# Self-attention of an adaLN cross block: adding the two chunks of weights on VectorE before the sum over keys

## The chip, the cores and the metric

The kernel runs on one core of one Trainium2 chip. The metric is the device time of one execution in microseconds (us); three runs of the kernel before gave 2964.05 us as their median, with 2962.16 and 2967.8 at the ends.

## The reference

All tensors are float32. There are B = 16 sequences of N = 224 tokens, width H = 512, 16 heads of 32, and a context of 750 tokens for each sequence. Cut to what matters:

```python
shift_a, scale_a, gate_a, shift_m, scale_m, gate_m = split(silu(c) @ W_mod + b_mod, 6)
x_norm = _ln(x) * (1 + scale_a) + shift_a
q, k, v = split(x_norm @ W_qkv + b_qkv, 3)              # 16 heads of 32
attn_w = softmax(einsum('bhqd,bhkd->bhqk', q, k) * scale)
attn_out = einsum('bhqk,bhkd->bhqd', attn_w, v)         # heads joined to 512
x = x + gate_a * (attn_out @ W_proj + b_proj)
# then cross-attention to the context, with weights softmax(q_c k_c^T),
x = x + (softmax(...) @ v_c) @ W_cproj + b_cproj
# then the MLP of width 2048
x = x + gate_m * (gelu((_ln(x)*(1+scale_m)+shift_m) @ W_mlp1 + b_mlp1) @ W_mlp2 + b_mlp2)
```

The change is in the softmax of the self-attention: `attn_w` is never formed. The kernel multiplies the unnormalised exponentials by `v`, sums them over the keys apart from that, and divides the first by the second.

## The kernel before, in words

The kernel has three stages that follow one another: self-attention (to about 770 us of the profiled span), cross-attention (to about 2290 us) and the MLP.

**Self-attention.** The 16 sequences go in 8 pairs `p`, and the 16 heads in 4 groups `g` of 4 heads (a group fills 128 rows of queries or keys, 32 for each head). A unit is one pair, one group and one sequence `j` of the pair, so there are 64 units. Keys lie on partitions, in TC = 2 chunks of TP = 112, and the 224 queries along the free dimension. For each unit:

1. `self_scores`: TensorE makes the scores with queries on partitions, VectorE takes the maximum of each query (`m`, one reduction over 112x1792) and splits it into bfloat16 parts (`split_max`, four small instructions, tile `nm`). `max_rows` turns them on TensorE, and VectorE copies the result (`mrow`).
2. `self_weights` (through `weights_t`): TensorE makes the scores again, now with keys on partitions, less the maximum, in PSUM tile `sc`. ScalarE takes the exponential into `pt`, 112 partitions x 4 heads x (2 chunks x 224 queries).
3. `self_values`: `values` multiplies `pt` by `v` with 8 matmuls of 32 columns (2 chunks x 4 heads) into the left half of PSUM tile `o`; `sums` multiplies `pt` by ones with another 8 such matmuls into its right half, so that every one of a head's 32 rows holds the sum over the keys.
4. `finish` (`normalize`): VectorE takes the reciprocal of the sums into `rinv` and multiplies the left half of `o` by it into `at`, which the projection reads.

Steps 2 to 4 run one unit behind step 1. In program order, one turn of the loop is: scores of this unit; `finish` of the unit two back; slot 0 of the plan; weights of the unit one back; `max_rows`; slot 1 of the plan; values and sums of the unit one back. The plan, a table keyed by pair, unit and slot, puts the projections of the next pair (`project_qk`, `project_v`, `turn_x`), the output projection of the pair before (`project`) and the norms between these steps. `sc` exists once (4 banks of PSUM), `o` once, `mm` three times, `pt` twice. Every instruction goes through `Ordered`, so each engine's instructions stand in the order in which the program issues them. All of them carry line 28 in the profile, the line of that helper, and are told apart by their tiles.

In pairs 0 to 6 a slot mostly holds 8 float32 matmuls. The last pair has no next pair to project for, and its plan spreads what is left in `halves`: slots there hold 4 or 8 matmuls.

`project` reads a `gate` tile, which `gate_rows` loads over SyncE's queue when a sequence's first chunk is projected; VectorE adds the bias (`upd`), and GpSimd multiplies by the gate and adds to `x`. The pool has 3 buffers of `gate` before.

**Cross-attention** runs similar units with 6 chunks of 125 keys. There GpSimd already adds all chunks into one tile `acc` (`Unit.weights`), and `sums` is called with that tile alone, so it is 4 matmuls. It uses `normalize` too. **The MLP** uses `gate_rows` with 3 buffers.

Of the kernel before, what the change touches and what calls it, by code (L numbers as in the profile page):

```python
# [8 lines left out]
F32 = mybir.dt.float32  # L9
BF16 = mybir.dt.bfloat16  # L10
AF = mybir.ActivationFunctionType
ALU = mybir.AluOpType
# [25 lines left out]
def kernel(  # L38
# [23 lines left out]
    nc = Ordered(tc)  # L62
    B, N, H = x.shape
    S = context.shape[1]
    MLP = w_mlp1.shape[1]
    P = 128
# [4 lines left out]
    HG = P // HD  # L71
    TP = 112
    TC = N // TP
    CP = 125
    CC = S // CP
# [5 lines left out]
    PN = PB * N  # L81
# [6 lines left out]
    NW = MLP // H  # L88
    NT = 3
    SCALE = float(HD) ** -0.5  # L90
    assert N == TC * TP and S == CC * CP and PN <= 512 and TC * N <= 512


    const = ctx.enter_context(tc.tile_pool(name="const", bufs=1))
# [19 lines left out]
    for i in range(3):  # L114
        t = const.tile([TP, TC, HG, HD], BF16, name=f"nm{i}")
# [86 lines left out]
                self.stats(i)  # L202
            self.apply()

    def gate_rows(pool, which, lo, n):

        g = pool.tile([n, H], F32, name="gate", bufs=3)
        at = lo
        while at < lo + n:
            b = at // N  # L210
            to = min((b + 1) * N, lo + n)
            nc.sync.dma_start(out=g[at - lo : to - lo, :], in_=gate_d[which][b].partition_broadcast(to - at))
            at = to
        return g

    def add_to_x(pool, ps, x_ap, bias, gate):
        r = ps.shape[0]
        t = pool.tile([r, H], F32, name="upd", bufs=2)
        nc.vector.tensor_tensor(t, ps, bias, ALU.add)
        if gate is not None:  # L220
            nc.gpsimd.tensor_tensor(t, t, gate, ALU.mult)
        nc.gpsimd.tensor_tensor(x_ap, x_ap, t, ALU.add)

    def project_heads(ps, a_t, w, lo):
        for g in range(KC):
            mm(ps[:TP, :H], a_t[g][:, lo : lo + TP], w[:, g, :], start=(g == 0), stop=(g == KC - 1))
            if g == 1:
                yield
# [6 lines left out]
    sa = self_pools.enter_context(tc.tile_pool(name="sa", bufs=3))  # L235
# [20 lines left out]
    for i in range(2):  # L256
        lo = (2 + 3 * i) * H
# [64 lines left out]
    def max_rows(pool, psum, nm):  # L322

        ps = psum.tile([P, 1024], BF16, name="mm")
        for c in range(TC):
            turn(ps[:, c * TP : (c + 1) * TP], nm[:, c].rearrange("p s d -> p (s d)"), ident16[:TP, :TP])
        row = pool.tile([P, N], BF16, name="mrow", bufs=2)
        nc.vector.tensor_copy(row, ps[:, :N])
        return row

    def weights_t(pool, psum, row, q_ap, k_ap, chunks, rows, bufs):

        st = psum.tile([P, HG, 512], F32, name="sc")
        n = len(chunks)
        for s in range(HG):
            mm(
                st[:rows, s, : n * N].rearrange("p (k t) -> p k t", k=n),
                ones16[s * HD : s * HD + NT, :rows],
                row[s * HD : s * HD + NT, :].unsqueeze(1).to_broadcast([NT, n, N]),
                start=True, stop=False,  # L340
            )
        for j, kc in enumerate(chunks):
            for s in range(HG):
                mm(
                    st[:rows, s, j * N : (j + 1) * N], k_ap(s, kc), q_ap(s),
                    start=False, stop=(j == n - 1),
                )
        pt = pool.tile([rows, HG, n * N], F32, name="pt", bufs=bufs)
        nc.scalar.activation(pt, st[:rows, :, : n * N], AF.Exp)
        return pt  # L350

    def values(o, pt, v_ap, chunks, rows, first):

        for j, kc in enumerate(chunks):
            for s in range(HG):
                mm(
                    o[s * HD : (s + 1) * HD, :N], v_ap(s, kc), pt[:, s, j * N : (j + 1) * N],
                    start=(first and j == 0), stop=False, skip_group_check=True,
                )

    def sums(o, pts, rows):

        for i, pt in enumerate(pts):
            for s in range(HG):
                mm(
                    o[s * HD : (s + 1) * HD, N : 2 * N], ones[:rows, :HD], pt[:, s, :],
                    start=False, stop=(i == len(pts) - 1), skip_group_check=True,
                )

    def normalize(pool, o, dst):  # L370
        rinv = pool.tile([P, N], F32, name="rinv", bufs=1)
        nc.vector.reciprocal(rinv, o[:, N : 2 * N])
        nc.vector.tensor_tensor(dst, o[:, :N], rinv, ALU.mult)

    def value_bias(pool, psum, w, vec, o_v, name):

# [9 lines left out]
    def run(plan, key):  # L386
        for f in plan.pop(key, ()):
            f()
# [19 lines left out]
    def load_ctx(b, hf):  # L408
        for c in range(hf * CH, (hf + 1) * CH):
            t = cw["cx"].tile([CP, H], F32, name="cx")  # L410
            nc.sync.dma_start(out=t, in_=context[b, c * CP : (c + 1) * CP, :])
            cx[b, c] = t
        ts = [cx[b, c] for c in range(hf * CH, (hf + 1) * CH)]
        cnorms[b, hf] = Norm(ts, ts, CP)
# [20 lines left out]
    if True:  # L435
# [6 lines left out]
        gate = {}  # L442
# [29 lines left out]
        def fetch(p):  # L472
            for b in range(PB * p, PB * (p + 1)):
                xs[b] = load_x(sa, tokens(x, b), 6)
# [15 lines left out]
        def project(p, t):  # L490
            b, c = PB * p + t // TC, t % TC
            if c == 0:
                gate[b] = gate_rows(sa, 0, b * N, TP)
            ps = ps_mm.tile([P, 512], F32, name="mm")
            yield from project_heads(ps, at[p], wproj, t * TP)
            add_to_x(sa, ps[:TP, :H], xs[b][:, c, :], bproj, gate[b])
            if c == TC - 1:
                nc.sync.dma_start(out=x_self[b], in_=xs[b])
# [7 lines left out]
        for p in range(NP):  # L506
# [23 lines left out]
            n = p + 1  # L530
# [35 lines left out]
        def self_weights(p, g, j, row):  # L566
            return weights_t(
                sa, ps_s, row,
                lambda s: qk[p, g][s * HD : (s + 1) * HD, j * N : (j + 1) * N],
                lambda s, kc: qk[p, KC + g][  # L570
                    s * HD : (s + 1) * HD, j * N + kc * TP : j * N + (kc + 1) * TP
                ],
                range(TC), TP, 2,
            )

        def self_values(p, g, j, pt):
            o = ps_o.tile([P, 512], F32, name="o")
            values(
                o, pt, lambda s, kc: vs[p, j * TC + kc][:, (g * HG + s) * HD : (g * HG + s + 1) * HD],
                range(TC), TP, True,  # L580
            )
            sums(o, [pt[:, :, c * N : (c + 1) * N] for c in range(TC)], TP)
            if g == 0 and j == 0:
                at[p] = []
            if j == 0:
                at[p].append(sa.tile([P, PN], F32, name="at", bufs=2 * KC))
            return lambda: normalize(sa, o, at[p][g][:, j * N : (j + 1) * N])
# [19 lines left out]
        was = None  # L607
        finish = None
        for i, (p, g, j) in enumerate(units):
            u = g * PB + j  # L610
            nm = nms[i % 3]
            self_scores(p, g, j, nm)
            if finish:
                finish()
            run(plan, (p, u, 0))
            if was:
                pt = self_weights(*was, row)
            row = max_rows(sa, ps_mm, nm)
            run(plan, (p, u, 1))
            if was:  # L620
                finish = self_values(*was, pt)
            was = (p, g, j)

            left = len(units) - i
            if left == 16:
                for hf in range(2):
                    load_ctx(0, hf)
                for c in range(TC):
                    first[c] = cw["mx"].tile([P, H], F32, name="mx")
                    nc.sync.dma_start(out=first[c][:TP], in_=x_self[0][:, c, :])  # L630
            if left in (10, 8):
                cnorms[0, left == 8].all()
            if left in (7, 6):
                Norm([first[7 - left][:TP]], [first[7 - left][:TP]], TP).all()
        finish()
        self_values(*was, self_weights(*was, row))()
        for t in range(PT):
            whole(project(NP - 1, t))
        assert not plan
# [163 lines left out]
    with tc.tile_pool(name="ca", bufs=2, reuse_waits="tile") as ca:  # L803
# [98 lines left out]
        for b in range(B):  # L902
            n = b + 1
# [52 lines left out]
        class Unit:  # L956
# [103 lines left out]
            def finish(self):  # L1060
                t = ca.tile([P, N], F32, name="at", bufs=2 * KC)
                normalize(ca, self.o, t)
                at.setdefault(self.b, []).append(t)
# [60 lines left out]
    with tc.tile_pool(name="ml", bufs=3, reuse_waits="tile") as ml:  # L1124
# [9 lines left out]
        resid = {}  # L1134
# [16 lines left out]
        def fetch(i):  # L1151
            t = ml.tile([P, H], F32, name="xr")
            q, lo = divmod(i * P, GR)
            nc.sync.dma_start(out=t, in_=x_cross[q][lo : lo + P, :])
            resid[i] = t, gate_rows(ml, 1, i * P, P)

        with (
            tc.tile_pool(name="ml_p", bufs=2, space=PSUM, reuse_waits="tile") as ps_p,
# [146 lines left out]
```

## Time and profile before

| | us |
|---|---|
| median of three runs | 2964.05 |
| lowest and highest | 2962.16, 2967.8 |
| the profiled execution, its time | 2967.63 |
| the profiled execution, its span | 2965.8 |
| TensorE matmuls busy | 2877.7 |
| VectorE busy | 1843.2 |
| ScalarE busy | 1175.4 |
| GpSimd busy | 1289.0 |

The span runs from the first to the last instruction; the execution's own time is 1.83 us longer, and lies 3.6 us above the median of the three runs. PE is TensorE's matmuls, PEld its weight loads, DVE VectorE, ACT ScalarE, POOL GpSimd, SP SyncE. A row of instructions gives the tile written, the tiles read, the shapes, the count, the busy time and the mean duration of one. A float32 matmul leaves two records, so 8 matmuls are shown as x16. In the timeline the first column is the start and the second the time until the last of the merged instructions ended; a bracket gives the idle time of the engine before it and what ended that.

### The profile page before, as it was taken

To read this page: it belongs to the slowest core of one execution; us is meant where nothing else is said; L and a number is where in the kernel's file an instruction comes from. 1 tells how busy PE (TensorE), PEld (TensorE's weight loads), DVE (VectorE), ACT (ScalarE), POOL (GpSimd) and SP (SyncE) were. 2 spreads that over 40 slices of the span, in tenths; PEclk is the share of its full clock that TensorE was granted. 3 is DMA by queue.
4 is the path that set the end of the run, shared out by engine and by line. 5 is a ranking of instruction groups with operands and counts; after the bars stand their busy time and mean duration, and the time that the engine had idled before them with its cause. 6 is when DMAs were issued, how large, how long until landed. Compare 5 with 4: busy or idle time off the path is not lost.

```text
span 2965.8 us, 47584 instructions
## 1 busy us (share of the span) xinstructions
PE 2877.7 (97%) x19901; PEld 1851.1 (62%) x19901; DVE 1843.2 (62%) x2624; ACT 1175.4 (40%) x1462; POOL 1289.0 (43%) x1636
## 2 busy tenths in 40 slices
PE   8999999999999999999999999999988999999999
PEld 5544444544455655555556556555655888888888
DVE  2556555566377777777777877877776633443343
ACT  1122121222356656656665666566553122112211
POOL 1022211122266766766767766667664510221021
PEclk9999999999999999999999999999999999999999
DMA  5111101100100101000011001010011211111110
GB/s 183 63 32 32 32 10 29 53 20 20 60 21 22 34 24 34 30 19 31 24 34 34 24 22 34 24 34 24 7 58 67 74 36 54 43 40 36 54 43 29
DMA packets 55387, 114.47 MB, mean 39 GB/s; under 512 B 4308, under 2 KB 4372, under 8 KB 55172
## 3 DMA queue, kind: packets, MB, share of 16 engines
q1 hardware_dynamic: 54560, 110.58, 11.6%
q8 instruction: 156, 2.56, 0.4%
q10 hardware_dynamic: 612, 0.85, 0.1%
q14 instruction: 59, 0.48, 0.1%
HBM read 89.33 MB, written 22.09 MB: 38 GB/s over the span
## 4 chain that ended last, share of the span: by engine, by line
PE 81%; DVE 7%; issue 4%; ACT 3%; POOL 3%; DMA 1%; SPq 0%; ACTq 0%; POOLq 0%; DVEq 0%
PE mm L28 46%; PE a L28 10%; PE sc L28 9%; PE o L28 9%; PE b L28 5%; ACT pt L28 3%; PE c L28 3%; DVE top L28 1%; POOL acc L28 1%; DVE rinv L28 1%; DVE stats L28 1%; DVE mc L28 1%; DVE m L28 1%; ACT kt L28 1%; POOL upd L28 0%
## 5 line engine op out<-in xcount | busy, mean ns | idle before, releaser
L28 POOL TENSOR_TENSOR acc<-acc,pt 125x448 f32<-125x448 f32 x512 | 585.1, 1143 | 40.2
L28 DVE TENSOR_TENSOR pt<-pt,o 125x896 f32<-125x896 f32 x384 | 394.3, 1082 | 92.1 <-PE o L28 87.0
L28 ACT COPY pt<-sc 125x1792 f32<-125x1792 f32 x192 | 317.5, 1654 | 223.3 <-DVE top L28 198.9
L28 DVE TENSOR_TENSOR top<-top,sc 125x896 f32<-125x896 f32 x320 | 346.6, 1083 | 40.7 <-PE sc L28 34.0
L28 POOL TENSOR_TENSOR upd<-upd,gate 112x512 f32<-112x512 f32 (+1 forms) x60 | 79.1, 1318 | 668.9 <-DVE upd L28 664.3
L28 PE MATMUL mm<-wkvc,cxt 128*125 128x512 f32 x768 | 354.4, 604 | 8.6 <-ACT kt L28 8.6
L28 PE MATMUL mm<-cxt,wkvc 128*128 128x375 f32 x1024 | 349.8, 484 | 2.4 <-ACT cxt L28 2.4
L28 ACT ACTIVATE pt<-pt 125x896 f32<-125x896 f32 x384 | 339.1, 955 | 12.6 <-DVE pt L28 11.9
L28 POOL TENSOR_TENSOR acc<-pt 125x448 f32<-125x448 f32 x128 | 146.6, 1146 | 380.3 <-ACT pt L28 380.3
L28 DVE RECIPROCAL rinv<-o 128x224 f32<-128x224 f32 x128 | 198.7, 1553 | 108.6 <-PE o L28 108.6
L28 PEld LDWEIGHTS mm<-cxt,wkvc 128*128 128x128 f32 x1024 | 190.1, 191 | 112.4 <-issue 12.8
L28 DVE TENSOR_REDUCE m<-sc 112x8 f32<-112x1792 f32 x64 | 129.7, 2026 | 209.4 <-PE sc L28 209.4
L28 ACT ACTIVATE pt<-sc 112x1792 f32<-112x1792 f32 x64 | 106.5, 1665 | 365.4 <-PE sc L28 365.4
L28 PEld LDWEIGHTS mm<-wkvc,cxt 128*125 128x125 f32 x768 | 136.5, 187 | 175.1 <-issue 153.5
L28 POOL TENSOR_TENSOR rstd<-mv,eps 112x2 f32<-112x2 f32 (+3 forms) x93 | 18.0, 194 | 475.7 <-DVE mv L28 475.7
L28 PE MATMUL sc<-qt,kt 32*125 32x224 f32 x3072 | 202.7, 378 | 12.9 <-ACT pt L28 12.3
L28 PE MATMUL mm<-xt,wqkv 128*128 128x448 f32 x512 | 209.6, 552 | 4.7 <-DVE xt L28 4.7
L28 PEld LDWEIGHTS sc<-qt,kt 32*125 32x125 f32 x3072 | 134.0, 184 | 92.9 <-issue 41.2
L28 ACT COPY mrow<-mm 128x896 bf16<-128x896 bf16 x64 | 58.0, 906 | 309.5 <-PE mm L28 309.5
L28 PE MATMUL o<-pt,vt 125*32 125x224 f32 x3072 | 158.5, 354 | 0.0
L28 PEld LDWEIGHTS mm<-xt,wqkv 128*128 128x128 f32 x512 | 92.5, 191 | 86.8 <-issue 81.0
L28 ACT COPY mx<-a 128x512 f32<-128x512 f32 x26 | 15.2, 586 | 325.1 <-POOL upd L28 306.3
(193 smaller groups left out, 4815.1 us busy)
## 6 DMA issues: line engine op xcount, KB each, us to landing
cx<-in_ctx_dram SPq DMA_DIRECT2D x96, 250.0 KB
x<-in_x_dram SPq DMA_DIRECT2D x16, 448.0 KB
x_self<-x SPq DMA_DIRECT2D x16, 448.0 KB
x<-x_self SPq DMA_DIRECT2D x16, 448.0 KB
x_cross<-x SPq DMA_DIRECT2D x16, 448.0 KB
mx<-x_cross SPq DMA_DIRECT2D x28, 256.0 KB
w<-in_L_xcond_W_mlp_dram SPq DMA_DIRECT2D x7, 1024.0 KB
xr<-x_cross SPq DMA_DIRECT2D x28, 256.0 KB
```

The costliest lines, as they stand in the source:

```text
L28: return lambda *args, **kw: self.tc.keep_in_program_order(f(*args, **kw))
```

## The change

VectorE adds the two chunks of `pt` into a tile `acc` (112 partitions x 4 heads x 224), once for each unit. The add stands behind `max_rows` and ahead of slot 1 of the plan. `sums` then gets `acc` alone, so it issues 4 matmuls and not 8; `values` still reads `pt`. In `normalize`, for self- and cross-attention, the reciprocal is written where the product is to stand, and the product is made in place, so `rinv` goes. The self-attention's pool keeps 2 buffers of `gate` and not 3; the MLP's call is told the 3 that it had.

```diff
-    assert N == TC * TP and S == CC * CP and PN <= 512 and TC * N <= 512
+    assert TC == 2 and N == TC * TP and S == CC * CP and PN <= 512 and TC * N <= 512
...
-    def gate_rows(pool, which, lo, n):
-        g = pool.tile([n, H], F32, name="gate", bufs=3)
+    def gate_rows(pool, which, lo, n, bufs):
+        g = pool.tile([n, H], F32, name="gate", bufs=bufs)
...
     def normalize(pool, o, dst):
-        rinv = pool.tile([P, N], F32, name="rinv", bufs=1)
-        nc.vector.reciprocal(rinv, o[:, N : 2 * N])
-        nc.vector.tensor_tensor(dst, o[:, :N], rinv, ALU.mult)
+        nc.vector.reciprocal(dst, o[:, N : 2 * N])
+        nc.vector.tensor_tensor(dst, o[:, :N], dst, ALU.mult)
...
-                gate[b] = gate_rows(sa, 0, b * N, TP)
+                gate[b] = gate_rows(sa, 0, b * N, TP, 2)
...
-        def self_values(p, g, j, pt):
+        def add_keys(pt):
+            acc = sa.tile([TP, HG, N], F32, name="acc", bufs=1)
+            nc.vector.tensor_tensor(acc, pt[:, :, :N], pt[:, :, N:], ALU.add)
+            return acc
+
+        def self_values(p, g, j, pt, acc):
...
-            sums(o, [pt[:, :, c * N : (c + 1) * N] for c in range(TC)], TP)
+            sums(o, [acc], TP)
...
             if was:
                 pt = self_weights(*was, row)
             row = max_rows(sa, ps_mm, nm)
+            if was:
+                acc = add_keys(pt)
             run(plan, (p, u, 1))
             if was:
-                finish = self_values(*was, pt)
+                finish = self_values(*was, pt, acc)
...
-        self_values(*was, self_weights(*was, row))()
+        pt = self_weights(*was, row)
+        self_values(*was, pt, add_keys(pt))()
...
-            resid[i] = t, gate_rows(ml, 1, i * P, P)
+            resid[i] = t, gate_rows(ml, 1, i * P, P, 3)
```

## The prediction

> **What bounds the kernel now.** I read the page's busy times first, then its chain of waits, then the busy times by stretch of self-attention, where nearly all of the change lies.
>
> ```profile
> PE 2877.7 (97%) x19901; PEld 1851.1 (62%) x19901; DVE 1843.2 (62%) x2624; ACT 1175.4 (40%) x1462; POOL 1289.0 (43%) x1636
> PE 81%; DVE 7%; issue 4%; ACT 3%; POOL 3%; DMA 1%; SPq 0%; ACTq 0%; POOLq 0%; DVEq 0%
> ...
> 210.00:310.00 100.00, 98.91 (x805) 49.42 (x798) 56.05 (x97) 21.04 (x19) 16.02 (x20) 1.00 0.09 24
> ```
>
> The last line is one stretch of 100 us: PE busy 98.91, PEld 49.42, DVE 56.05, ACT 21.04, POOL 16.02, clock 1.00. TensorE sets the pace, at full clock, and VectorE is free 44% of the time. Work taken from TensorE here should come off the time, if nothing makes TensorE wait. Whether it does is read from one unit. The timeline of its second half, without weight loads:
>
> ```profile
> 302.90 1.66 ACT L28 ACTIVATE pt<-sc 112x1792 f32<-112x1792 f32 x1 [0.60 <-PE sc L28]
> 303.00 0.27 DVE L28 COPY mrow<-mm 128x224 bf16<-128x224 bf16 x1
> ...
> 306.38 0.96 PE L28 MATMUL o<-pt,v 112*32 112x224 f32 x16
> ...
> 307.16 0.94 PE L28 MATMUL o<-pt,ones 112*32 112x224 f32 x16
> ...
> 308.03 1.02 PE L28 MATMUL sc<-qk 32*112 32x224 f32 x16
> ...
> 309.12 2.03 DVE L28 TENSOR_REDUCE m<-sc 112x8 f32<-112x1792 f32 x1 [5.84 <-PE sc L28]
> ```
>
> The exponential ends at 304.56, and the sums over keys start at 307.16, 2.60 us later, because 8 projection matmuls and the values lie between. VectorE has nothing to do from 303.27 to 309.12. So there is room for an add exactly where the change puts it.
>
> **The change part by part.**
>
> *Sums: 8 matmuls become 4, 64 times.* Values start at 306.38 and sums at 307.16, 0.78 us for 16 records; sums take 0.87 us until the next scores start, which includes the switch to another shape of tile. What 4 matmuls and that switch cost can be read in cross-attention, where `sums` already gets one tile:
>
> ```profile
> 1512.18 2.48 PE L28 MATMUL o<-pt,vt 125*32 125x224 f32 x48
> 1514.47 0.56 PE L28 MATMUL o<-acc,ones 125*32 125x224 f32 x8
> 1514.96 1.04 PE L28 MATMUL sc<-qt,kt 32*125 32x224 f32 x16
> ```
>
> They take 1514.96 - 1514.47 = 0.49 us. So 0.87 - 0.49 = 0.38 us go for each unit at full clock; 2.29/48 x 8 = 0.38 from the row above says the same. Where the clock is halved, as in the first unit (sums from 71.35 to 73.00, 1.65 us) and the last two (739.07 to 740.72 and 746.19 to 747.84), it is up to 0.82.
>
> *The add, 64 times.* Its row does not exist yet. The nearest by shape and engine:
>
> ```profile
> L28 DVE TENSOR_TENSOR pt<-pt,o 125x896 f32<-125x896 f32 x384 | 394.3, 1082 | 92.1 <-PE o L28 87.0
> ```
>
> 896 elements, two inputs: 1.08 us. But there one input is in PSUM, and the add has both in SBUF. In the MLP, adds with two SBUF inputs beside GpSimd look so:
>
> ```profile
> 2319.55 0.92 DVE L28 TENSOR_TENSOR s<-h,h 128x512 f32<-128x512 f32 x1
> ...
> 2319.87 1.73 POOL L28 TENSOR_TENSOR ws<-w 128x512 f32<-128x512 f32 x1
> 2320.50 1.65 DVE L28 TENSOR_TENSOR h<-h 128x512 f32<-128x512 f32 x1
> ```
>
> The 128x512 add takes 1.65 us beside GpSimd; the quietest of that size, 0.68 (`tt<-mxt`). The Trainium skill has the rule: "SBUF — State Buffer", section "Who interferes with whom", says that a VectorE instruction with two SBUF inputs contends with a GpSimd instruction that reads SBUF, that the lock is exclusive, and that whoever comes second waits for the other to end. It speaks against this change. By the row alone the add takes 1.08 everywhere; by the rule, 1.08 plus what is left of a GpSimd instruction when the exponential ends. I went through all 64 units. GpSimd runs then in 14 that matter: units 0 and 2 (of 8) of pairs 1 to 6, and two of the last pair. Each time the gate product has 0.28 us left and the addition to `x` follows after 0.08. So the add ends 1.36 us after the exponential, or, if GpSimd wins the second turn too, 1.62 + 1.08 = 2.70. I take the first: in the MLP rows the engines alternate.
>
> *Who waits for the add.* TensorE's sums do, with about 0.06 us on each side (the exponential ends at 675.56, values start at 675.62), so they can start 1.20 after the exponential. Before they started this long after it: 2.60 us in units 0, 2, 4 and 5 of a pair, 2.18 in 1, 6 and 7, 4.27 in 3. In unit 1 the copy of `mrow` ends up to 0.7 after the exponential, so the add is done at 1.85, still under 2.18. So in units 1 to 54 the add is hidden by the projection matmuls of slot 1, the 12 contended ones included (1.48 against 2.60; if GpSimd wins twice, 2.76, a loss of 0.16 x 12 = 1.9 us in all). What cover is left is 0.3 to 3 us.
>
> Behind the add in VectorE's queue stand the evictions of slot 1 (`upd`, `xt`), which wait for TensorE 2.0 and 3.2 us after the exponential anyway, and norm statistics, which end before the next `m` reduction: its idle time is at least 1.06 us.
>
> The last pair is different: most of its second slots hold 4 matmuls, and values start as soon as the exponential ends. One unit, with GpSimd at work:
>
> ```profile
> 700.84 1.66 ACT L28 ACTIVATE pt<-sc 112x1792 f32<-112x1792 f32 x1 [7.62 <-PE sc L28]
> ...
> 701.51 1.27 POOL L28 TENSOR_TENSOR upd<-upd,gate 112x512 f32<-112x512 f32 x1 [6.41 <-DVE upd L28]
> ...
> 702.60 0.96 PE L28 MATMUL o<-pt,v 112*32 112x224 f32 x16
> ...
> 702.86 1.28 POOL L28 TENSOR_TENSOR x<-x,upd 112x512 f32<-112x512 f32 x1
> ...
> 703.38 0.94 PE L28 MATMUL o<-pt,ones 112*32 112x224 f32 x16
> ```
>
> The exponential ends at 702.50, sums start 0.88 later. With the add ready at 0.28 + 1.08 + 0.12 = 1.48 they wait 0.60, and the unit loses 0.22 net. Units 55 to 61 have 0.83 to 0.89: those without contention wait 0.31 to 0.37 and gain 0.01 to 0.07. In unit 55 three pairs of statistics (2.5 us) stand behind the add, so the next reduction starts about 0.9 late, which its slot of 8 matmuls hides, but the next add ends later too: unit 56 loses about 0.1. The seven sum to -0.3 us; if GpSimd wins twice in the two contended ones, -3. The last two units, at half clock, have 1.55 between exponential and sums: the add fits, and 0.82 comes off each.
>
> *The rest.* The reciprocal (1.55 us) and product (0.39) stay, 128 of each; in place costs nothing I can find (`pt<-pt,o` is in place and shows 1082 for 896 elements, in line with 392 for 224). The reciprocal now is what waits for an `at` buffer, 1.55 us earlier, but those are reused two pairs (in cross-attention two sequences) later, after their projection. A gate load now needs the gate two back, not three: the last goes out at 759.84, and the one two back was read until 729.97. The SyncE queue keeps its order; nothing moves past anything. The pools' layout shifts by under 1 KB; one copy at the hand-over to cross-attention (769.36, after a GpSimd addition) could start up to 1 us earlier or later. Off both ends I take zero.
>
> *Sum.* Units 1 to 54: 54 x 0.38 = 20.5. Unit 0: 0.4 to 0.8, since what stays runs at half clock for longer; 0.5. Units 55 to 61: -0.3. Units 62 and 63: 1.6. Together 22.3 us off the profiled execution: 2967.63 becomes 2945.3, its span 2943.5. That execution lies 3.6 us above the median of the runs, so I expect 2964.05 - 22.3 = 2941.7, 0.75% faster.
>
> **The rivals.**
>
> *Partly hidden gain* (8%). GpSimd wins the lock more often than I think, or the add takes nearly 2 us. Then units 1, 6 and 7 just fit or lose 0.1 and each unit of the last pair loses over 0.8: 22.3 - 3 - 7 = about 12 us, 2952. For: MLP adds doubled. Against: GpSimd is busy 16% here, and idle in 50 of the units' windows.
>
> *The add becomes what TensorE waits for* (5%, slower). The place is the first sums matmul, the mechanism VectorE's add under a lock or at another price. It decides when the add exceeds about 2.4 us: there eight units of a main pair wait 1.7 of the 3.0 that they save, which leaves 9 us over 55 units, and the last pair's seven lose 1.3 each, as much. The worst 128x512 row of this kind in the trace is 2.82 us (`ws<-ws,w` beside GpSimd). With 2.82 for the add, sums wait 0.34 in four units of eight, 0.76 in two and 1.45 in unit 1, 4.3 against 3.0 gained; over 55 units a loss of 9, the last pair some 12 more: 2983. Against it: those rows ran beside a GpSimd that never paused.
>
> *The sums do not shrink* (4%, no change). If the 0.87 us were set by loading weights and the switch, halving the matmuls would free little: 2961 to 2964. The 0.49 in cross-attention speaks against it.
>
> **How the numbers follow.** The forecast has 83%. A difference under 0.2%, 5.9 us, is about what a measurement here cannot tell from none. Faster by more: the forecast and most of the second case, 0.90; same 0.05; slower 0.05. The forecast's own range: 0.36 to 0.41 a unit (19.5 to 22), -3 to +1 in the last pair, the hand-over and clock +-1, and 2 to 3 us by which medians of few runs differ: 2935 to 2948. The range reaches to 2949, to take in part of the second case.
>
> **What would show it.** Right: `o<-acc,ones` with 512 records in place of 1024 `o<-pt,ones`; from its start to the next scores 0.49 us; `acc<-pt` near 1.08 us, longest where GpSimd multiplies by the gate; TensorE's rows without a wait for `acc` before unit 55 and waits of 0.3 to 0.6 after; self-attention about 22 us shorter, cross-attention and MLP as long as before. Wrong: waits of TensorE for `acc` in pairs 0 to 6, an `acc` row over 2.2 us, a later `m` reduction with TensorE idle behind it, or a longer cross-attention.

## The result and the profile after

| | before | changed |
|---|---|---|
| median of four runs, us | 2965.53 | 2944.2 |
| lowest and highest | 2962.16, 2967.8 | 2940.97, 2946.7 |
| the profiled execution, time and span | 2967.63, 2965.8 | 2940.97, 2939.2 |

The ratio is 0.9929, with a 95% interval of 0.9914 to 0.9944: 21.3 us less, where 22.3 was forecast. The changed kernel was run again beside the later experiments:

> The changed kernel itself once more, beside the variants of this call. Expected: 0.7% faster than before, 2941 to 2947 us; the span of its profile may differ by 4 to 5 us between runs, all of it in units 0 to 2, where TensorE's clock is at half for one spell or two.

It gave 2942.33 us against 2962.76, 20.4 us less (four and fifteen runs, ratio 0.9925, 0.9911 to 0.9939).

The profiled executions lie 26.6 us apart and not 21. TensorE's granted clock is at half for one or two spells between 66 and 95 us, in different places and for different lengths from one profiled execution to the next: 13.8 us together in the one of before, 6.9 in the one of the changed kernel. Half of the difference, 3.4 us, is an estimate of what this adds to the distance. The profile shown of before was a long one; the times of one kernel, changed or not, spread over 5 to 8 us. Below, units are compared from unit 3 on, where these spells are past.

The page's busy times and its chain of waits, then the stretch from 210 to 310 us (span, then busy PE, PEld, DVE, ACT and POOL, clock):

```profile
PE 2850.1 (97%) x19389; PEld 1829.9 (62%) x19389; DVE 1913.6 (65%) x2688; ACT 1175.4 (40%) x1462; POOL 1296.2 (44%) x1636
PE 80%; DVE 8%; issue 4%; ACT 4%; POOL 3%; DMA 1%; SPq 0%; ACTq 0%; POOLq 0%; DVEq 0%
...
210.00:310.00 100.00, 98.91 (x772) 49.51 (x765) 69.39 (x112) 20.51 (x18) 17.44 (x20) 1.00 0.08 24
```

TensorE has 512 records less, and in the stretch it is as busy as before, 98.91 of 100 us: it gets further in the same time and waits no more than before. VectorE went from 56 to 69 of 100 us. Up to unit 54 none of the 64 adds stands in the chain of waits; from unit 55 on, eight of the last nine do. Now the unit that the prediction showed, in the changed kernel:

```profile
290.03 1.66 ACT L28 ACTIVATE pt<-sc 112x1792 f32<-112x1792 f32 x1 [0.55 <-PE sc L28]
290.19 0.28 DVE L28 COPY mrow<-mm 128x224 bf16<-128x224 bf16 x1
291.73 1.09 DVE L28 TENSOR_TENSOR acc<-pt 112x896 f32<-112x896 f32 x1 [1.26 <-ACT pt L28]
293.57 0.96 PE L28 MATMUL o<-pt,v 112*32 112x224 f32 x16
...
294.35 0.56 PE L28 MATMUL o<-acc,ones 112*32 112x224 f32 x8
294.84 1.03 PE L28 MATMUL sc<-qk 32*112 32x224 f32 x16
```

Sums start at 294.35 and the next scores at 294.84: 0.49 us, where it was 0.87. The add is ready at 292.82, 1.53 us before the sums. (The counts of projection matmuls given ahead, 8 or 4 in a slot, are counts of records: a slot holds 4 or 2 matmuls. No time depends on it.) The groups of the self-attention stretch, with the mean of one in ns behind the busy time:

```profile
L28 DVE TENSOR_TENSOR acc<-pt 112x896 f32<-112x896 f32 x64 | 72.1, 1126 | 38.1 <-ACT pt L28 37.6
...
L28 PE MATMUL o<-acc,ones 112*32 112x224 f32 x512 | 37.3, 361 | 1.3 <-DVE acc L28 1.0
```

The second row's last part is TensorE's idle time for the add: little, and all of it from unit 55 on. The timeline of the unit of the last pair that the prediction showed:

```profile
675.92 1.27 POOL L28 TENSOR_TENSOR upd<-upd,gate 112x512 f32<-112x512 f32 x1 [4.16 <-DVE upd L28]
676.88 1.26 DVE L28 TENSOR_TENSOR acc<-pt 112x896 f32<-112x896 f32 x1 [0.86 <-ACT pt L28]
677.01 0.96 PE L28 MATMUL o<-pt,v 112*32 112x224 f32 x16
677.27 2.00 POOL L28 TENSOR_TENSOR x<-x,upd 112x512 f32<-112x512 f32 x1
...
678.19 0.59 PE L28 MATMUL o<-acc,ones 112*32 112x224 f32 x8 [0.22 <-DVE acc L28]
678.71 1.03 PE L28 MATMUL sc<-qk 32*112 32x224 f32 x16
```

Two things are to be seen. The add takes 1.26 us and not 1.09, and GpSimd's addition to `x` behind it 2.00 and not 1.28: it looks as if each held the other up, and the fifth experiment below tests that. And the sums start 1.18 us after the values and not 0.78. The idle time in the bracket, 0.22, is only part of that wait, since the previous matmuls' records reach into it.

### The profile page after: what moved, and what is told of

Its sections match the earlier page's. It is cut to its first block, busy times and chain, and to the rows that moved or that the text cites. A ratio compares the mean times of both kernels' runs of the same rounds, so it can differ in the third digit from the quotient of the medians.

```text
span 2939.2 us, 46558 instructions
## 1 busy us (share of the span) xinstructions
PE 2850.1 (97%) x19389; PEld 1829.9 (62%) x19389; DVE 1913.6 (65%) x2688; ACT 1175.4 (40%) x1462; POOL 1296.2 (44%) x1636
## 4 chain that ended last, share of the span: by engine, by line
PE 80%; DVE 8%; issue 4%; ACT 4%; POOL 3%; DMA 1%; SPq 0%; ACTq 0%; POOLq 0%; DVEq 0%
PE mm L28 46%; PE a L28 10%; PE sc L28 9%; PE o L28 8%; PE b L28 5%; ACT pt L28 3%; PE c L28 3%; DVE at L28 2%; DVE top L28 2%; POOL acc L28 1%; DVE stats L28 1%; DVE m L28 1%; DVE mc L28 1%; ACT kt L28 1%; DMA gate<-gate_d 1%
## 5 line engine op out<-in xcount | busy, mean ns | idle before, releaser
L28 DVE RECIPROCAL at<-o 128x224 f32<-128x224 f32 x128 | 198.8, 1553 | 102.1 <-PE o L28 102.1
```

What stands on the lines that cost most here:

```text
L28: return lambda *args, **kw: self.tc.keep_in_program_order(f(*args, **kw))
```

## The experiments

**The add without the shorter sums.** The question is what part of the change the gain belongs to.

```diff
-            sums(o, [acc], TP)
+            sums(o, [pt[:, :, c * N : (c + 1) * N] for c in range(TC)], TP)
```

> The changed kernel, but the sums go back to 8 matmuls over pt; the add is still made and nothing reads acc. Theory (the gain is the four TensorE matmuls taken away, 0.38 us for each unit; the add costs something only where TensorE waits for it): sums to next scores 0.87 us as before, no wait for acc, the last pair a few tenths slower because VectorE's statistics come later; the whole within 2 us of the kernel before. Rival A (the gain comes from the reciprocal in place or from the smaller pools): about 20 us faster than before. Rival B (the add takes time from TensorE through VectorE's queue also in pairs 0 to 6): 10 us or more slower than before.

Measured: 2963.73 us against 2962.87, ratio 1.0003 (0.9994 to 1.0011). Its sums, in the timeline:

```profile
303.46 0.94 PE L28 MATMUL o<-pt,ones 112*32 112x224 f32 x16
304.33 1.03 PE L28 MATMUL sc<-qk 32*112 32x224 f32 x16
```

0.87 us again, in every unit from 3 to 61 (unit 56 apart, 0.90). The 64 adds alone cost nothing that the runs can tell, and without the matmuls gone there is no gain. Both rivals fall.

**The reciprocal in place and two gate buffers alone.** The kernel before, with the new `normalize` and `bufs=2` for the self-attention's gates.

> The kernel before with the reciprocal in its result's place and 2 gate buffers, no add, 8 matmuls for the sums. Theory: within 2 us of before, unit by unit the same. Rival A (the gain comes from here): about 20 us faster.

Measured: 2962.68 us against 2962.87, ratio 1.0002 (0.9994 to 1.0011). From unit 4 to unit 61 it stands against before by the same 4.3 us, which the first units set, mostly by their spells of half clock. This part of the change is worth nothing that the runs can tell, as costed.

**The short sums without the add.** What does the add cost, then?

```diff
-            sums(o, [acc], TP)
+            sums(o, [pt[:, :, :N]], TP)
...
-            if was:
-                acc = add_keys(pt)
```

> The changed kernel without the add: the sums run over the first chunk of keys alone, in 4 matmuls, so the second chunk is left out of the divisor. Theory: as the changed kernel, plus what the add costs in the last pair: its seven units with full clock wait 0.1 to 0.5 us for acc each, some 2.5 us together with the late statistics, so 2 to 4 us faster than the changed kernel, about 24 us (0.8%) faster than before. Rival (the add costs nothing anywhere): equal to the changed kernel, unit by unit. Rival B (the add costs in all pairs): 10 us or more faster than the changed kernel.

Measured: 2943.43 us, ratio 0.9932 (0.9919 to 0.9946); the runs do not set it apart from the changed kernel, and its profiled execution has a longer spell of half clock in units 0 to 2. Unit by unit it is clear. From unit 4 to 55 the two kernels keep their distance within 0.02 us, so there the add is free. From 55 to 61 this kernel gains 2.2 us (its distance goes from -3.48 to -1.30). A unit in which the changed kernel waits for `acc`:

```profile
653.40 0.96 PE L28 MATMUL o<-pt,v 112*32 112x224 f32 x16
...
654.18 0.56 PE L28 MATMUL o<-pt,ones 112*32 112x224 f32 x8
...
654.68 1.02 PE L28 MATMUL sc<-qk 32*112 32x224 f32 x16
```

Values to sums 0.78, as everywhere in the main pairs; with the add it is 1.13 in this unit. So both rivals fall as well: the add costs something, and only in the last pair. The gain of 2 to 4 us that was expected in the whole time did not come out of the spread.

**The add made twice.** This tests the cover itself: how much more would the place bear?

```diff
             nc.vector.tensor_tensor(acc, pt[:, :, :N], pt[:, :, N:], ALU.add)
+            nc.vector.tensor_tensor(acc, pt[:, :, :N], pt[:, :, N:], ALU.add)
```

> The changed kernel with the add made twice in a row into acc. Theory (cover of 2.66 us from exponential to sums in units 0, 2, 4, 5 of a pair, 2.24 in 1, 6, 7, 4.34 in 3, and 0.8 to 0.9 in the last pair): acc is ready 2.27 us after the exponential, 2.5 in unit 1. Sums wait about 0.3 in unit 1 and up to 0.05 in 6 and 7 of pairs 0 to 6, 3 us in all; about 1.4 in place of 0.35 in units 55 to 61, 7 to 9 us; 0.7 in each of the last two. Together 11 to 14 us slower than the changed kernel, so 0.25 to 0.35% faster than before. Rival (covered everywhere): equal to the changed kernel. Rival B (VectorE bounds): 64 x 1.09, 70 us slower.

Measured: 2975.31 us, ratio 1.0044 to before (1.0031 to 1.0057). That is 12.4 us slower than before, where the changed kernel run again was 20.4 us faster than before: some 33 us between the two, not 11 to 14. The expectation was right in units 1 and 3 to 7 (waits of 0.1 in 6 and 7, 0.3 in 1) and wrong in 0 and 2. The timeline of a unit 0:

```profile
158.22 3.29 DVE L28 TENSOR_TENSOR acc<-pt 112x896 f32<-112x896 f32 x2
158.56 2.00 POOL L28 TENSOR_TENSOR x<-x,upd 112x512 f32<-112x512 f32 x1
...
160.02 0.96 PE L28 MATMUL o<-pt,v 112*32 112x224 f32 x16
...
161.57 0.58 PE L28 MATMUL o<-acc,ones 112*32 112x224 f32 x8 [0.58 <-DVE acc L28]
```

Elsewhere two adds take 2.22; here 3.29, and 3.64 in unit 2. The first add goes ahead of GpSimd's addition, which then takes its turn, and the second add ends only after that. The expectation had no wait in these units; the sums start 1.55 us after the values and not 0.78, so it costs 0.8 us in unit 0, and 1.1 in unit 2, 11.5 us over the six pairs. In the last pair the sums wait 1.4 to 1.5 us, as expected, but 2.5 in the two contended units, and there the clock falls to half as well (the sums of unit 61 take 0.90). That this is GpSimd's doing was so far only a coincidence in time, and the next experiment tried it.

**Two adds, and no GpSimd in the way.**

```diff
-            add_to_x(sa, ps[:TP, :H], xs[b][:, c, :], bproj, gate[b])
+            nc.vector.tensor_tensor(xs[b][:, c, :], ps[:TP, :H], bproj, ALU.add)
```

> The kernel with two adds, without GpSimd's part in self-attention's projection: VectorE writes projection plus bias straight into x, so the gate and the residual of self-attention are left out. Theory (the second add is held by GpSimd's addition to x, which takes the lock first): the two adds take 2.2 us in every unit, also in units 0 and 2 of a pair, where they took 3.3 to 3.6; sums wait 0 there in place of 0.8 and 1.1, 11 us less over six pairs, and 2 to 8 us less in units 58 and 61 with what follows of the clock: 2956 to 2964 us. Rival (those units are late for another reason, the eviction of the projection in VectorE's queue): as with GpSimd, 2973 to 2978.

Measured: 2959.05 us against 2962.76, ratio 0.9987 (0.9978 to 0.9995), within the expectation. All adds into `acc`, over the stage (minimum, median, maximum in ns), with two adds and GpSimd, and then without GpSimd:

```profile
L28 DVE TENSOR_TENSOR acc<-pt x128: 1081/1093/2054, 66.5 to 755.1; 112x896 f32<-112x896 f32 x128
```

```profile
L28 DVE TENSOR_TENSOR acc<-pt x128: 1076/1091/1094, 65.7 to 737.9; 112x896 f32<-112x896 f32 x128
```

No add is held any more, and the sums of units 0 and 2 start 0.78 after the values, with no wait, as in this unit 0:

```profile
155.68 0.96 PE L28 MATMUL o<-pt,v 112*32 112x224 f32 x16
...
156.46 0.56 PE L28 MATMUL o<-acc,ones 112*32 112x224 f32 x8
```

Six pairs give 9.1 us and not 11, because unit 1 now loses 0.3 to 0.4: its adds start 0.6 to 0.7 us after the exponential and not 0.24, behind VectorE's norm statistics. Units 58 and 61 give 3.7 more. The rival, a late eviction, falls: VectorE's eviction still stands in its queue. These 12.8 us are most of the 16.3 between the medians of the two kernels; the rest is not traced to a unit (in these two profiles units 0 to 2 differ by 4.3 more, in the spells of half clock).

**The sums behind the next scores, in all units.** The cover in the last pair is too short by 0.35 us, and 0.97 us of scores follow the sums. So they were exchanged.

```diff
-            return lambda: normalize(sa, o, at[p][g][:, j * N : (j + 1) * N])
+            return lambda: sums(o, [acc], TP), lambda: normalize(sa, o, at[p][g][:, j * N : (j + 1) * N])
...
             self_scores(p, g, j, nm)
             if finish:
+                add_up()
                 finish()
```

> The changed kernel with the 4 sum matmuls issued behind the next unit's scores, in all units, so that the add has another 0.97 us of cover. Theory: no wait for acc is left in units 55 to 61, 2.2 us less (the amount by which the kernel without the add passed those units sooner). But values and sums are no longer neighbours with the same tile shape: if the switch between the 32-column and the 32-row tiles costs the 0.1 us that the sums showed beyond their 0.38, every unit pays it once more, 64 x 0.1 = 6 us, and the whole is 3 to 5 us slower than the changed kernel. Rival (the switch costs nothing, the 0.1 us is the sums' own start): 2 us faster than the changed kernel.

Measured: 2946.03 us, ratio 0.9942 (0.9928 to 0.9956), 3.7 us above the changed kernel run beside it, within the 3 to 5 that the theory gave. The timeline:

```profile
296.06 0.96 PE L28 MATMUL o<-pt,v 112*32 112x224 f32 x16
...
296.96 1.03 PE L28 MATMUL sc<-qk 32*112 32x224 f32 x16
297.91 0.59 PE L28 MATMUL o<-acc,ones 112*32 112x224 f32 x8
...
298.43 1.77 PE L28 MATMUL mm<-xt,wqkv 128*128 128x448 f32 x4
```

From values to the projection it takes 298.43 - 296.06 = 2.37 us; in the changed kernel 295.80 - 293.57 = 2.23. The other switch of tile shape costs 0.14 us, 0.13 to 0.15 in seven units of a pair; unit 3 gains 0.4, which the theory did not have. Against the profile of the changed kernel run beside it, 3.9 us are lost from unit 4 to unit 55 and 1.6 won in units 55 to 61. That leaves 2.3; the other 1.4 us between these two profiles come behind self-attention, where the kernels do the same, so that the total of 3.7 fits so well is in part chance.

**The same in the last pair alone.** The late sums only for units 55 to 61.

> As the kernel before this one, but the sums are put behind the next scores only in units 55 to 61, where TensorE waits for acc. Theory: 2.2 us of waits go and 0.7 of switches come: units 55 to 61 take 1 to 2 us less than in the changed kernel, pairs 0 to 6 are the same unit by unit. That is too little to tell from the runs' times (0.05%); the trace of the last pair decides. Rival (the waits are put off to VectorE's queue: statistics behind the add delay the next maximum, so TensorE waits there): no gain in those units.

Measured: 2941.89 us, ratio 0.9925 (0.9913 to 0.9938); the changed kernel beside it 2942.33. Pairs 0 to 6 are the same. Units 55 to 60 gain 0.8, which speaks against the rival there, and unit 61 loses 0.67 of it in the profiled execution, where the clock fell to half at about 704 us. So of the 1 to 2 us expected 0.1 is left, and that execution cannot say whether the loss in unit 61 is chance. A gain in the whole time is not shown. A detail of the contended units, from the kernel with late sums in all units:

```profile
154.48 1.26 POOL L28 TENSOR_TENSOR x<-x,upd 112x512 f32<-112x512 f32 x1
154.60 2.09 DVE L28 TENSOR_TENSOR acc<-pt 112x896 f32<-112x896 f32 x1 [0.58 <-ACT pt L28]
```

In this unit the exponential ends 0.1 us after GpSimd's addition has begun. So the add waits for all of it and takes 2.09 us, and GpSimd keeps its 1.26. In the changed kernel the add starts 0.38 us before GpSimd's addition, while the gate product still runs, and the bill goes the other way: 1.25 and 2.00.

## Why the prediction was right

*The bound.* TensorE carried the stage: busy 98.91 of 100 us before and after, and shorter by what was taken from it.

*0.38 us a unit.* From cross-attention's own sums, 0.49 us for 4 matmuls with the switch behind them. Measured 0.49. The distance of the two kernels grew from 6.07 us at unit 3 to 25.70 at unit 55, 19.6 us over 52 units, 0.378 each. In units 0 to 2 the forecast can't be read, since the spells of half clock fell differently.

*The add.* The row of 1.08 us with one input in PSUM held for two inputs in SBUF: 1.08 to 1.09 in 50 units. In the 14 contended ones the prediction weighed the Trainium skill's lock ("SBUF — State Buffer", "Who interferes with whom") and took 1.36 us. They took 1.25 to 1.26, of which 0.17 is waiting and not 0.28: when the add starts, the record of the gate product has 0.30 us left, so either the product gives way some 0.1 us before its record ends, or that record is inexact. The second turn went to VectorE in the changed kernel, as taken from the MLP rows. That was in part luck: it hangs on which of the two comes first, by 0.38 us here, and the last experiments show it going the other way.

*The cover.* No wait for `acc` before unit 55. For units 55 to 61 the prediction's terms are +0.01 to +0.07 in each of 55, 57, 59 and 60, about -0.1 in 56, -0.22 in 58 and by the same rule -0.27 in 61; they add up to -0.4 and not to the -0.3 that it gives. Measured, for units 55 to 61 in order: +0.07, -0.23, +0.12, -0.05, +0.07, +0.11, -0.40, together -0.3. That the sum fits is luck. Unit 61 lost so much because the clock fell to half before it ended (at about 709.6 us); in the profile of the changed kernel run again it did not, unit 61 lost 0.10, and the seven came to 0.0. Unit 56 lost more than thought, since `nm` came late and the transposes waited for it: the reduction `m` started 0.65 us later behind the exponential of unit 55 than before the change, since the statistics stand ahead of it, and two of the small instructions took longer beside GpSimd (0.54 and 0.63 us; before the change one did, 0.45).

*The last two units.* Forecast 0.82 each at half clock. Unit 62 gained 0.86. Unit 63 gained 1.36, since the clock was back at full for part of it; in the profile of the changed kernel run again, with half clock in both, they gained 0.81 and 0.75. *The hand-over and the rest.* The store of sequence 14 is issued 27.1 us sooner and the end comes 26.6 us sooner, so what follows self-attention is 0.5 us longer, within the 1 us allowed for.

*The rivals.* The sums did shrink. The partly hidden gain did not come. The slower one did not come with one add, but its mechanism is real: two adds, 2.22 us alone and 3.3 to 3.6 beside GpSimd, are 0.44% slower than before. Its turning point, an add of about 2.4 us in every unit, was not tried as such; two adds of 2.22 us in every unit, without GpSimd's part, were still 0.13% faster than before (ratio 0.9987), which fits it.

## What to carry to other kernels

Where TensorE is busy without a gap and VectorE waits, work moved from one to the other is worth what the moved matmuls cost by their own starts (0.38 us here, read from a place in the same trace that already had the short form), and the moved work is free as long as it ends before its first reader would have started. Measure that room in every unit, not in one: from the end of the exponential to the sums it was 2.2 to 4.3 us in the main pairs and 0.8 in the last, and only the last paid. VectorE's add with two inputs in SBUF had two prices beside GpSimd's addition, 1.25 and 2.09 us, according to which of the two started first, so cover such an instruction for the higher one.

## What the runs showed of the hardware

- VectorE's add with two SBUF inputs and GpSimd's addition exclude each other: 1.09 us alone, 1.25 when it starts with 0.30 us of a GpSimd product left, 2.09 when it starts 0.1 us after a GpSimd addition has begun; GpSimd's addition takes 2.00 and not 1.27 when it comes second. Without GpSimd's part in the projection all 128 adds took 1.08 to 1.09.
- Very small instructions of VectorE took longer beside GpSimd as well: behind unit 55 of the changed kernel, one that normally takes 0.18 us (`nm`) took 0.54 beside GpSimd's normalisation and ended with it. Here the cause is read from the coincidence in time alone.
- Between matmuls on 32-column tiles and on 32-row tiles TensorE loses 0.1 to 0.14 us: 0.49 less 0.38 behind the sums, and 0.14 for one more switch in each unit.
- The granted clock fell to half also where TensorE had no gap: in the profile of before it was 0.59 on average from 70 to 75 us, with TensorE busy 5.00 of 5.00 us. No run tried why.
